# Cross-attention on one Trainium2 core: seven block products in place of eight, values made directly, fixed buffers and a new order

## The chip, the core and the metric

The kernel runs on one core of one Trainium2 chip. The core has five instruction queues that work side by side: PE (TensorE, the matrix multiplier, with its weight loads listed as PEld), DVE (VectorE), ACT (ScalarE), POOL (GpSimd) and SP (SyncE, here only issuing DMA). Matrix products land in PSUM, eight banks of 128 partitions by 512 fp32 values. PE, DVE and ACT reach PSUM in this kernel; POOL works on SBUF alone. Each engine runs its own instructions strictly in the order in which the program lists them, and waits for the other engines through semaphores.

The metric is the device time of one execution in microseconds (us). Three executions of the kernel before took 1933.29, 1933.73 and 1934.09 us, with a median of 1933.73 us.

## The reference

Cut to what matters, with `B = 32` batches, `C = 256` channels and `N = 1024` positions:

```python
x_q = einsum('oc,bcn->bno', w_qk, y)
x_k = einsum('oc,bcn->bon', w_qk, x)
x_v = einsum('oc,bcn->bon', w_v, x) + b_v[None, :, None]
energy = einsum('bnc,bcm->bnm', x_q, x_k)
attention = softmax(energy, axis=-1)
attention = attention / (1e-07 + attention.sum(axis=1, keepdims=True))
x_r = einsum('bcn,bnm->bcm', x_v, attention)
x_r = relu(einsum('oc,bcn->bon', w_t, x - x_r) + b_t[None, :, None])
return x + x_r
```

## The kernel before, in words

**Weights folded once.** The program computes G = w_qk^T w_qk (negated) at the start, so that the keys of a batch are G x and the energies are y^T (G x); and w_t w_v, so that the output projection is folded into the values. All fp32 operands are split into two fp32r parts, HIGH (the rounded value) and LOW (the rest), and every product is three matmuls: HIGH x HIGH, HIGH x LOW, LOW x HIGH (`ORDER`, line 45). ACT writes the HIGH part as a copy, and DVE (if the source is in PSUM) or POOL (if it is in SBUF) writes the LOW part as a subtraction.

**One batch.** With channels as two blocks of 128 (`KC`), positions as two halves of 512 (`MB`) and eight position tiles of 128 (`NT`), a batch consists of these groups of matmuls, each of 128x128 weights against 128x512 columns unless said otherwise:

- `k`, keys G x: 2 output blocks x 2 halves x 2 input blocks x 3 = 24 (`keys`, `channels`, lines 287 to 301).
- `E`, energies: 8 tiles x 2 halves x 2 blocks x 3 = 96 (`energy`, line 357).
- `A`, attention: 8 tiles x 2 channel blocks x 2 halves x 3 = 96 (`attention`, line 413).
- `X`, w_t x: 24 (`straight`, line 339).
- `W`, the mixing of the attention result with w_t w_v: 24 (`mixed`, line 275). In batches 1 to 30 the attention works on x itself, turned to positions-by-channels through a strided load and a transpose on DVE (`load_positions`, `turned_x`, lines 233 to 262), and `W` follows. The first and the last batch have instead values made ahead, `V` (`values`, line 323): 48 matmuls of 128x256.

**Softmax of one tile** (lines 371 to 411): DVE takes the row minimum of the 128x1024 energies in PSUM (`min`), ACT does the exponential in place with the row sum (`exp`), DVE the reciprocal (`ri`), ACT the HIGH part of each half (`h`), DVE the LOW part (`l`) and the column sums (`sum`). At the batch's end DVE reduces the column sums (`cols`, `inv`, `turn`), scales the result (`div`), POOL adds w_t x (`join`), ACT applies ReLU (`pos`), a POOL DMA adds x from HBM (`add`) and an SP DMA stores (`st`).

**PSUM.** Banks are used as four pairs. Energies of successive tiles alternate between two pairs (`place`, line 354), so the next tile is multiplied while the softmax of this one runs; the other two pairs hold the attention result.

**Order.** Nothing reorders the work: the strings `FIRST`, `STEADY` (run for batches 2 to 30) and `STEPS` (lines 724 to 877) list the operations, one word each, and every engine takes its own words in that order. A `+` puts a word one batch ahead, a `-` one batch back.

Of the kernel before, what the change touches and what calls it, by code (L numbers as in the profile page):

```python
# [17 lines left out]
def kernel(  # L18
# [28 lines left out]
    const = ctx.enter_context(tc.tile_pool(name="const", bufs=1))  # L47
    ps_m = ctx.enter_context(tc.tile_pool(name="ps_m", bufs=1, space=bass.MemoryType.PSUM))
    one = ctx.enter_context(tc.tile_pool(name="one", bufs=1))
    yp = ctx.enter_context(tc.tile_pool(name="yp", bufs=3))  # L50
    ep = ctx.enter_context(tc.tile_pool(name="ep", bufs=3))
    rawp = ctx.enter_context(tc.tile_pool(name="rawp", bufs=4))
    xep = ctx.enter_context(tc.tile_pool(name="xep", bufs=3))
    sp = ctx.enter_context(tc.tile_pool(name="sp", bufs=3))
# [20 lines left out]
    banks = ps_m.tile([P, 8, MB], F32, name="banks")  # L75

    def pair(j):
        return banks[:, 2 * j : 2 * j + 2]

# [6 lines left out]
    def accumulate(into, from_):  # L86
        return pool.dma_start(into, from_, accum_op=ALU.add)

    stage = one.tile([P, KC, N], F32, tag="z", name="stage")

    def two(j):
        return stage.rearrange("p k n -> p (k n)")[:, 2 * j * C : 2 * (j + 1) * C].rearrange(
            "p (k c) -> p k c", k=KC
        )  # L100
# [5 lines left out]
    for k, start in enumerate((load, act.dma_start)):  # L106
        start(wqk[:, k], w_qk[ts(k, P)])

    def raw(name):
        return rawp.tile([P, N], F32, tag="raw", name=name)  # L110

    def raw_x(name, b, k, by=load):
        to = raw(f"{name}_{b}_{k}")
        by(to, x[b, ts(k, P)])
        return to

    def y_half(b, half):
        return y[b].rearrange("(k p) n -> p k n", p=P)[:, :, ts(half, MB)]

    x0 = [raw_x("x", 0, 0)]  # L120
    act.dma_start(wt, w_t.rearrange("(k p) c -> p k c", p=P))
    load(wv, w_v.rearrange("(k p) c -> p k c", p=P))
    x0.append(raw_x("x", 0, 1))

    few = const.tile([P, P], F32, name="few")
    zeros = nc.const_aps.tensor(0.0, [P, P], F32)
    parts = const.tile([P, NB, NG + 1], F32, name="parts")
    dve.memset(parts[:, :, NG], EPS)
    sc = const.tile([P, NB, 1], F32, name="sc")
    ubias = const.tile([P, KC, 1], F32, name="ubias")  # L130
    xbias = const.tile([P, KC, 1], F32, name="xbias")
    for _ in range(5):
        pe.matmul(banks[:, 7, :P], zeros, zeros, start=True, stop=True)
    make_identity(nc, ident)

    def positions(name):
        return xep.tile([P, N], F32, tag="xe", name=name)

    works = [positions(f"work_{j}") for j in range(2)]

    def work(j):
        return works[j // 2][:, ts(j % 2, KC * C)]

    def area(j):
        return work(j).rearrange("p (k c) -> p k c", k=KC)

    class Weights:

        def __init__(self, name, p, by):
            self.forms = const.tile([P, FORMS, KC, C], F32R, name=name)  # L150
            self.p, self.by = p, by
            self.h, self.l = (self.forms[:, j] for j in range(FORMS))

        def high(self, at=slice(0, KC)):
            act.mul(self.h[:, at], self.p[:, at], self.by)

        def low(self):
            dve.scalar_tensor_tensor(self.l, self.p, self.by, value(self.h), ALU.mult, ALU.subtract)

    def matmul(into, lhs, rhs, start, stop):  # L160
        pe.matmul(into, lhs, rhs, start=start, stop=stop, skip_group_check=True)

    def late(b):

        return 0 < b < B - 1

    class Queries:

        def __init__(self, q):
            self.b, self.half = divmod(q, MH)  # L170
            self.from_ = raw(f"y_{self.b}_{self.half}")
            load(self.from_.rearrange("p (k n) -> p k n", k=KC), y_half(self.b, self.half))

        def ordered(self, f):

            if late(self.b):
                return f.rearrange("p t k (g j) -> p (k g) t j", j=G32)
            return f.rearrange("p t k n -> p k t n")

        def loaded(self):  # L180
            if late(self.b):
                return self.from_.rearrange("p (h t j) -> p h t j", t=HT, j=G32)
            return self.from_.rearrange("p (k t n) -> p k t n", k=KC, t=HT)

        def high(self):
            self.f = yp.tile([P, FORMS, HT, KC, P], F32R, tag="yf", name=f"yf_{self.b}_{self.half}")
            act.copy(self.ordered(self.f[:, HIGH]), self.loaded())

        def low(self):
            pool.tensor_tensor(  # L190
                self.ordered(self.f[:, LOW]),
                self.loaded(),
                self.ordered(value(self.f[:, HIGH])),
                ALU.subtract,
            )
# [12 lines left out]

    class Batch:

        def __init__(self, b):
            self.b = b
            self.at = b % 2
            self.late = late(b)
            self.row, self.ef, self.uf, self.zf, self.xe = {}, {}, [], [], {}
            self.key_bank, self.x_from, self.xr, self.xp = {}, {}, {}, {}

        def load_x(self, k):
            self.xr[k] = raw_x("x", self.b, k)

        def x_high(self, k):
            if k == 0:
                self.xf = one.tile([P, FORMS, KC, N], F32R, tag="xf", name=f"xf_{self.b}")
            act.copy(self.xf[:, HIGH, k], self.xr[k])

        def x_low(self, k):
            pool.tensor_tensor(
                self.xf[:, LOW, k], self.xr[k], value(self.xf[:, HIGH, k]), ALU.subtract
            )

        def load_positions(self, q):
            self.xp[q] = raw(f"xp_{self.b}_{q}")
            to = self.xp[q].rearrange("p (c n) -> p c n", n=P)
            from_ = x[self.b].rearrange("(c r) n -> r c n", r=G32)
            for g in range(NG):
                load(to[ts(g, G32)], from_[:, :, q * MB + g * P : q * MB + (g + 1) * P])

        def turned_x(self, q):  # L240

            blocks = self.xp[q].rearrange("p (j r) -> p j r", r=G32)
            dve.transpose(blocks, blocks)

        def turned(self, q):
            return self.xp[q].rearrange("p (c t r) -> p t c r", t=HT, r=G32)

        def turned_form(self, q, j):
            return self.uf[q][:, j].rearrange("p (t c r) -> p t c r", t=HT, r=G32)

        def turned_high(self, q):
            u = one.tile([P, FORMS, HT * C], F32R, tag=f"uf{q}", name=f"uf_{self.b}_{q}")
            self.uf.append(u)
            act.copy(self.turned_form(q, HIGH), self.turned(q))

        def turned_low(self, q):
            pool.tensor_tensor(
                self.turned_form(q, LOW),
                self.turned(q),
                value(self.turned_form(q, HIGH)),  # L260
                ALU.subtract,
            )

        def mixed_high(self, k):
            f = ep.tile([P, FORMS, N], F32R, tag="ef", name=f"zf_{self.b}_{k}")
            self.zf.append(f)
            act.copy(f[:, HIGH], flat(pair(2 + k)))

        def mixed_low(self, k):
            f = self.zf[k]
            dve.tensor_tensor(f[:, LOW], flat(pair(2 + k)), value(f[:, HIGH]), ALU.subtract)

        def mixed(self, c, halves=range(MH)):
            for h in halves:
                for j, m in ORDER:
                    for k in range(KC):
                        matmul(
                            pair(3 - c)[:, h],  # L280
                            vw.forms[:, j, k, ts(c, P)],
                            self.zf[k][:, m, ts(h, MB)],
                            (j, m) == ORDER[0] and k == 0,
                            (j, m) == ORDER[-1] and k == KC - 1,
                        )

# [627 lines left out]
```

## Time and profile before

The profiled execution took 1933.57 us; its span, from first to last instruction, is 1931.4 us.

| engine | busy us | share of the span | instructions |
|---|---|---|---|
| PE | 1923.8 | 100% | 8553 |
| PEld | 1595.9 | 83% | 8553 |
| DVE | 1473.3 | 76% | 2083 |
| ACT | 1068.2 | 55% | 1485 |
| POOL | 665.8 | 34% | 331 |

Busy time is the union of an engine's instructions. A line of a group of instructions reads: program line, engine, operation, output<-input, shape, count, then the total busy time, the mean time of one instruction in ns, and the idle time of the engine just before them with what ended it. Matmuls are pipelined, so the mean time of one (389 ns for 512 columns) is longer than the distance between two. All calls go through one helper, so every row has line L67, and the names of the tiles tell the groups apart.

### The profile page before, as it was taken

The page shows a single profiled execution, that of the slowest core. Times are in us where ns is not written, and L with a number is a line of the kernel's source. Part 1 is how long each engine was busy: PE and PEld are TensorE (multiplying, and loading weights), DVE is VectorE, ACT ScalarE, POOL GpSimd, SP SyncE. Part 2 cuts the span into 40 slices and gives each one's busy share as a digit, 9 for nine tenths or more (in the row PEclk, how much of TensorE's full clock was granted, in tenths as well). Part 3 has the DMA queues.
Part 4 walks back from the last instruction along what each step waited for, and adds up shares of the span by engine and source line. Part 5 has one row for each costly group of instructions (what it writes and reads, how often), then busy time and mean ns, then how long its engine had stood idle before and what let it go on. Part 6 is the DMA issues. An engine that isn't in the chain of part 4 may idle for free.

```text
span 1931.4 us, 22944 instructions
## 1 busy us (share of the span) xinstructions
PE 1923.8 (100%) x8553; PEld 1595.9 (83%) x8553; DVE 1473.3 (76%) x2083; ACT 1068.2 (55%) x1485; POOL 665.8 (34%) x331
## 2 busy tenths in 40 slices
PE   9999999999999999999999999999999999999998
PEld 8888888888888888888888888888888888888887
DVE  6877877778777787777877778877778777787776
ACT  6555555555555555555555555555555555555544
POOL 3333234232343333333333333334233342323413
PEclk9999999999999999999999999999999999999999
DMA  4133234332243322434224333233332343322321
GB/s 139 57 97 88 66 88 109 87 98 67 77 109 88 102 66 73 109 88 109 71 63 107 99 98 86 58 97 101 96 88 64 90 109 88 91 63 87 109 55 44
DMA packets 112126, 168.08 MB, mean 87 GB/s; under 512 B 8336, under 2 KB 70928, under 8 KB 112016
## 3 DMA queue, kind: packets, MB, share of 16 engines
q1 hardware_dynamic: 102960, 134.77, 22.8%
q0 software_dynamic: 8640, 31.46, 9.4%
q8 instruction: 67, 1.10, 0.2%
q14 instruction: 43, 0.35, 0.1%
q10 hardware_dynamic: 416, 0.39, 0.1%
HBM read 133.04 MB, written 33.55 MB: 86 GB/s over the span
## 4 chain that ended last, share of the span: by engine, by line
PE 99%; DMA 0%; DVE 0%; issue 0%; ACT 0%
PE banks L67 99%; DMA stage<-in_L_xattn_w_qk_dram 0%; DVE banks L67 0%; DVE z L67 0%; ACT work L67 0%
## 5 line engine op out<-in xcount | busy, mean ns | idle before, releaser
L67 PE MATMUL banks<-ef,uf 128*128 128x512 f32 x3051 | 731.0, 388 | 0.0
L67 PE MATMUL banks<-gf,yf 128*128 128x512 f32 x3072 | 728.6, 389 | 0.0
L67 PEld LDWEIGHTS banks<-gf,yf 128*128 128x128 f32 x3072 | 576.4, 188 | 119.5
L67 PEld LDWEIGHTS banks<-ef,uf 128*128 128x128 f32 x3051 | 571.4, 188 | 118.1
L67 ACT ACTIVATE banks<-banks,nm 128x1024 f32<-128x1024 f32 x256 | 278.7, 1089 | 399.3 <-DVE nm L67 398.8
L67 DVE TENSOR_REDUCE nm<-banks 128x1 f32<-128x1024 f32 x256 | 313.6, 1225 | 209.4 <-PE banks L67 205.9
L67 ACT ACTIVATE ef<-banks,ri 128x512 fp32r<-128x512 f32 x506 | 323.9, 686 | 184.9 <-DVE ri L67 108.8
L67 DVE SCALAR_TENSOR_TENSOR ef<-banks,ri,ef 128x512 fp32r<-128x512 f32 x506 | 370.4, 743 | 13.2 <-ACT ef L67 12.0
L67 POOL TENSOR_TENSOR uf<-xp,uf 128x1024 fp32r<-128x1024 f32 x60 | 144.5, 2409 | 603.9 <-ACT uf L67 597.5
L67 DVE SCALAR_TENSOR_TENSOR acc<-banks,ri,acc 128x512 f32<-128x512 f32 x448 | 327.9, 744 | 5.0 <-ACT ef L67 0.2
L67 POOL TENSOR_TENSOR z<-z,xe 128x1024 f32<-128x1024 f32 (+1 forms) x63 | 150.8, 2394 | 205.0 <-DVE z L67 187.3
L67 POOL TENSOR_TENSOR xf<-x,xf 128x1024 fp32r<-128x1024 f32 x62 | 149.2, 2407 | 168.8 <-ACT xf L67 168.8
L67 PE MATMUL banks<-xf,gw 128*128 128x512 f32 x768 | 189.3, 389 | 0.0
L67 PE MATMUL banks<-xf,tw 128*128 128x512 f32 x768 | 184.3, 389 | 0.0
L67 POOL TENSOR_TENSOR yf<-y,yf 128x1024 fp32r<-128x1024 f32 x64 | 163.7, 2559 | 17.1 <-ACT yf L67 17.1
L67 PEld LDWEIGHTS banks<-xf,tw 128*128 128x128 f32 x768 | 144.1, 188 | 29.9
L67 PEld LDWEIGHTS banks<-xf,gw 128*128 128x128 f32 x768 | 144.1, 188 | 29.8
L67 PE MATMUL banks<-zf,vw 128*128 128x512 f32 x720 | 168.2, 389 | 0.0
L67 PEld LDWEIGHTS banks<-zf,vw 128*128 128x128 f32 x720 | 135.1, 188 | 28.1
L67 DVE TENSOR_TENSOR zf<-banks,zf 128x1024 fp32r<-128x1024 f32 x60 | 73.4, 1225 | 104.9 <-ACT zf L67 104.9
L67 POOL DMA_DIRECT2D z<-in_x_dram x60 | 52.6, 876 | 240.5 <-ACT z L67 240.5
L67 ACT CAST gf<-banks 128x1024 fp32r<-128x1024 f32 x64 | 64.9, 1016 | 100.0 <-PE banks L67 100.0
(76 smaller groups left out, 1001.6 us busy)
## 6 DMA issues: line engine op xcount, KB each, us to landing
x<-in_x_dram SPq DMA_DIRECT2D x64, 512.0 KB, 4.1
y<-in_ctx_dram SPq DMA_DIRECT2D x64, 512.0 KB, 3.9
out_dram<-z SPq DMA_DIRECT2D x62, 512.0 KB, 2.7
xp<-in_x_dram SPq DMA_DIRECT2D x240, 128.0 KB, 3.0
z<-in_x_dram POOLq DMA_DIRECT2D x60, 512.0 KB, 6.6
xo<-in_x_dram SPq DMA_DIRECT2D x4, 512.0 KB, 3.4
out_dram<-z SPq DMA_DIRECT2D x3, 256.0 KB, 2.0
stage<-in_L_xattn_w_t_dram ACTq DMA_DIRECT2D x1, 256.0 KB, 4.8
```

The costliest lines, as they stand in the source:

```text
L67: self.last = getattr(self.engine, name)(*args, **kwargs)
```

## The change

Nearly the whole program is rewritten. What is computed stays the same; these are the parts.

**Seven block products.** Keys, w_t x and energies become chains of seven products of blocks (Strassen's scheme in Winograd's form) in place of eight, each product again three matmuls. For the energies a pair of position tiles p (tiles 2p and 2p+1) is one chain: 2 tiles x 2 channel blocks on the left, 2 channel blocks x 2 halves on the right. The products accumulate in three PSUM banks: bank a takes P1, P6, P7, P4 in turn, bank b P2, bank c P5 and P3. Between them the partial sums of bank a are read out by ACT (`r1` after P1, `r2` after P6, `r3` after P7) and added by DVE into the other banks:

```python
def product(into, left, right, first):
    for i, (j, m) in enumerate(ORDER):
        matmul(into, left(j), right(m), first and i == 0, i == len(ORDER) - 1)
...
def chain(name, bank, left, right):
    where = {1: "a", 2: "b", 5: "c", 6: "a", 7: "a", 4: "a", 3: "c"}
    for i, w in where.items():
        words[f"{name}P{i}"] = lambda b, i=i, w=w: product(
            banks[:, bank[w]], left(i), right(i), i in (1, 2, 5)
        )
...
KB = dict(a=2, b=0, c=1)
...
XB = dict(a=6, b=4, c=5)
...
EB = dict(a=2, b=0, c=1, d=3)
...
def energy_read(b, p, j):
    act.copy(rs["e", b, p, j], eb["a"])

def energy_block(b, p, j, w, to, least, first):
    dve.tensor_tensor_reduce(
        out=eb[to], in0=eb[w], in1=rs["e", b, p, j], scale=1.0,
        scalar=LARGE if first is None else small[first, b, p],
        op0=ALU.add, op1=ALU.min, accum_out=small[least, b, p],
    )

def energy_least(b, p):
    dve.tensor_reduce(small["mD", b, p], eb["a"], AX.X, ALU.min)
    dve.tensor_tensor(small["m1", b, p], small["mD", b, p], small["mB", b, p], ALU.min)

def tile_banks(n):
    return banks[:, EB["a"] : EB["a"] + 2] if n % 2 else banks[:, EB["b"] : EB["b"] + 2]
...
word(f"E{p}c11", energy_block, p, 1, "b", "b", "mA", None)
word(f"E{p}c22", energy_block, p, 3, "c", "d", "mB", None)
word(f"E{p}c12", energy_block, p, 2, "c", "c", "m0", "mA")
word(f"E{p}m21", energy_least, p)
```

So `c11` is bank b plus r1, `c22` is bank c plus r3 written to bank d, `c12` is bank c (after P3) plus r2; the row minimum comes out of the same instructions and of `m21`, which reduces bank a and combines two columns of one value per row (`m1`). Tile 2p lies in banks 0 and 1, tile 2p+1 in banks 2 and 3, and every pair of every batch, and the keys (`KB`), use these same banks. Attention, values and w_t x use banks 4 to 7.

**Operands.** Left and right operands of the seven products are four blocks as they are and sums of blocks. The sums are made before the split: on POOL for x (`xT1` to `xT4`) and y (`ys1` to `ys4` of each half), on DVE and POOL for the keys (`kT1`, `kT3`, `kT4` and `kT2`). Their HIGH parts are further ACT copies (`xTh`, `ysh`, `kTh`) and their LOW parts further POOL subtractions (`xTl`, `ysl`, `kTl`); the key blocks' own HIGH and LOW (`khD`, `klD`) are an ACT copy and a POOL subtraction, since `kc11` and `kc22` put them in SBUF. For the weights this is done once (`left_blocks`), for G on DVE, for w_t on POOL.

**Values.** Every batch makes `V` (48 matmuls of 128x256), split by `vh` on ACT and `vl` on DVE. The turned load, its transpose and `W` are gone.

**Buffers.** Pools that rotate are replaced by one tile per buffer: one set of x, y, key and value operands, one z and one xe (w_t x), two raw input tiles, four attention tiles (`efs`), four tiles of sums and four of reads (`rs`).

**Order.** New strings. The steady one, for batch b, begins and goes on:

```
+xTl1 +yl01 +ys13 sum61 A400 A511 +kr1 h61 +kP6 +ysl0 +ys12 sum60 l60 +kr2 +kP2
l61 +kP7 +kP5 A700 -add0 +yl00 +ys14 h71 +kr3 +kP4 cols +kc11 +kc22 +kP3 l71 A600
+kc12 +khD +kT1 +kT3 A410 A501 A411 A710 A401 +kTh0 +kh21 +ysh1 +klD +kT2 +kTl0
inv +kT4 +kl21 turn A711 A610 +kTh1 A611 A701 +E0P1 +E0P2 +E0r1 +kTl1 +yl11 +E0P6
A601 +E0r2 +E0P7 -st0 +E0P5 div1 +E0c11 div0 +E0r3 +yh10 +E0c22 +E0P4 +E0P3 +E0m21
+V10 +yl10 +V11 +E0c12 join1 +exp1 +ri1 +exp0 +V00 +h10 +sum10 +sum11 +ri0 +l10
+h00 +E1P1 +l00 +vh1 ++ldx0 +sum01 +h11 +ysl1 +E1r1 +V01 +h01 +vl1 +vh0 +sum00
+E1P6 +xP1 +E1r2 ++ldx1 +E1P2 join0 ++xT3 +l11 +E1P7 +l01 +E1P5 +xr1 ++xh0 +E1r3
+vl0 +xP6 pos1 +E1c11 +E1P4 +E1c22 +xr2 +xP2 +E1m21 +exp3 +xc11 +E1P3 +E1c12 +ri3
+xP5 +A100 +h30 ++xl0 add1 ++xT1 +sum30 +exp2 +l30 +xP7 +A111 +sum31 +E2P1 +A011
...
+E2c22 +E2m21 +E2c11 +exp5 +ri5 +A101 +A311 +E2P3 +A000 +h50 +sum50 +l50 +E3P1
++xTh0 +A001 +E2c12 +h51 +E3r1 +exp4 ++ys01 ++xT2 ++ys03 +sum51 ++xT4 +A310 +E3P6
+ri4 +h41 +sum41 ++xl1 +A210 +A300 +E3r2 +E3P7 ++xTl0 ++ys02 ++ys04 ++xTh1 +h40
+A211 +l41 +sum40 +l51 +l40 +E3P5 +E3r3 +E3P4 +E3P2 +E3c22 ++ldy1 +E3P3 +A510
+E3m21 pos0 +E3c11 ++yh00 ++ysh0 +E3c12 +A301 +exp7 +ri7 +A200 +h70 +A201 ++ys11
+sum70 +l70 +exp6 ++yh11 +sum71 +A500 ++kP1 +ri6 st1 +h60
```

The start and the end are new too. The keys of the first batch, which ran as soon as G was there (`first_keys`), now come after the blocks of both weights, the bias product and the sums of x:

```
ldx0 ldx1 xT1 xh0 xl0 xT2 xh1 xl1 xT4 xTh1 xT3 xTl1 xTh0 xTl0 V00 V11 kP1 ldy0 kr1
kP6 V10 kP5 ldy1 yh11 kr2 yh01 ys01 kP2 kP7 kr3 ys03 yh00 kc22 kc11 V01 kP3 kP4
yl01 ys02 khD yl00 kc12 kT1 ys04 klD kh21 vh1 vh0 ysh0 kT3 vl1 kT2 kT4 kTh0 kl21
kTh1 vl0 E0P2 +ldx0 ysl0 kTl1 xP1 E0P1 xP2 xP5 E0r1 yh10 xr1 E0P6 xP6 kTl0 E0r2
...
```

The special last batch (`STEPS` with its `end_` functions, which split the last piece, kept x in SBUF and stored in pieces of 192 to 512 columns) is replaced by the steady operations in a short string:

```
A511 A501 A410 A411 A400 h71 A710 -add0 h61 sum60 sum61 l71 cols l60 inv l61 -st0
A711 A401 A700 A610 A611 A701 A601 turn A600 div1 div0 join1 join0 pos1 add1 pos0
st1 add0 st0
```

More of the change, by code (lines that the diff above doesn't have):

```diff
@@ new lines, with matmul @@
+    raws = Ring("raws", 2, [N])
+    sums = Ring("sums", 4, [2, MB])
+    efs = Ring("efs", 4, [FORMS, MH, MB], F32R)
+    rs = Ring("rs", 4, [MB])
+    small = Ring("small", 60, [1])
+    parts = mem.tile([P, NB, NG + 1], F32, name="parts")
+    sc = mem.tile([P, NB, 1], F32, name="sc")
+    ubias = mem.tile([P, KC, 1], F32, name="ubias")
+    xbias = mem.tile([P, KC, 1], F32, name="xbias")
+    wtb = mem.tile([P, KC], F32, name="wtb")
+    def matmul(into, lhs, rhs, start, stop):
+        pe.matmul(into, lhs, rhs, start=start, stop=stop, skip_group_check=True)
@@ L122 @@
[L122 to L133, printed above, removed]
@@ L160, in matmul @@
[L160 to L195, printed above, removed]
@@ L609 @@
[L609 to L621 removed]
+    zeros = nc.const_aps.tensor(0.0, [P, P], F32)
+    dve.memset(parts[:, :, NG], EPS)
@@ L622 @@
+    for _ in range(5):
+        pe.matmul(banks[:, 7, :P], zeros, zeros, start=True, stop=True)
+    make_identity(nc, ident)
+    gram(pair(2), wqk)
+    act.mul(graw[:, 0], pair(2)[:, 0, :C], -1.0)
+    act.mul(graw[:, 1, P:], pair(2)[:, 1, P:C], -1.0)
+    pe.transpose(pair(2)[:, 1, :P], graw[:, 0, P:], ident)
+    act.copy(graw[:, 1, :P], pair(2)[:, 1, :P])
+    left_blocks("g", gws, graw, dve)
     for i in range(KC):
@@ new lines @@
+    word("kc22", key_block, 3, "c", 1)
+    word("kc12", key_block, 2, "c", None)
+    word("kh21", lambda b: act.copy(g(HIGH, K21), kb["a"]))
+    word(
+        "kl21",
+        lambda b: dve.tensor_tensor(g(LOW, K21), kb["a"], value(g(HIGH, K21)), ALU.subtract),
+    )
+    word("kT1", key_sum, ("k13", 0), "c", ("k", 0))
+    word("kT3", key_sum, ("k13", 1), "c", ("k", 1))
+    word(
+        "kT2",
+        lambda b: pool.tensor_tensor(
+            sums["k24", b][:, 0], sums["k", b][:, 1], sums["k13", b][:, 0], ALU.subtract
+        ),
+    )
@@ new lines, with columns @@
+    for n in range(NT):
+        word(f"exp{n}", exp, n)
+        word(f"ri{n}", recip, n)
+        for h in range(MH):
+            word(f"h{n}{h}", high, n, h)
+            word(f"l{n}{h}", low, n, h)
+            word(f"sum{n}{h}", share, n, h)
+            for c in range(KC):
+                word(f"A{n}{c}{h}", attention, n, c, h)
+    def columns(b):
+        dve.tensor_reduce(
+            parts[:, :, 0],
+            acc.rearrange("p (j r) -> p j r", r=G32),
+            AX.X,
+            ALU.add,
+            apply_transpose=True,
+        )
@@ new lines, in divided, with joined, relu, added @@
+    def divided(b, c):
+        dve.scalar_tensor_tensor(z[:, c], flat(pair(2 + c)), ubias[:, c], rc, ALU.add, ALU.mult)
+    def joined(b, c):
+        pool.tensor_tensor(z[:, c], z[:, c], xe[:, c], ALU.add)
+    def relu(b, c):
+        act.activation(z[:, c], z[:, c], AF.Relu)
+    def added(b, c):
+        pool.dma_start(z[:, c], x[b, ts(c, P)], accum_op=ALU.add)
+    def stored(b, c):
+        load(out[b, ts(c, P)], z[:, c])
+    word("cols", columns)
+    word("inv", inverse)
+    word("turn", inverse_turned)
@@ new lines @@
+    """
+    STEADY = """
+        +xTl1 +yl01 +ys13 sum61 A400 A511 +kr1 h61 +kP6 +ysl0 +ys12 sum60 l60 +kr2 +kP2
+        l61 +kP7 +kP5 A700 -add0 +yl00 +ys14 h71 +kr3 +kP4 cols +kc11 +kc22 +kP3 l71 A600
+        +kc12 +khD +kT1 +kT3 A410 A501 A411 A710 A401 +kTh0 +kh21 +ysh1 +klD +kT2 +kTl0
+        inv +kT4 +kl21 turn A711 A610 +kTh1 A611 A701 +E0P1 +E0P2 +E0r1 +kTl1 +yl11 +E0P6
+        A601 +E0r2 +E0P7 -st0 +E0P5 div1 +E0c11 div0 +E0r3 +yh10 +E0c22 +E0P4 +E0P3 +E0m21
+        +V10 +yl10 +V11 +E0c12 join1 +exp1 +ri1 +exp0 +V00 +h10 +sum10 +sum11 +ri0 +l10
+        +h00 +E1P1 +l00 +vh1 ++ldx0 +sum01 +h11 +ysl1 +E1r1 +V01 +h01 +vl1 +vh0 +sum00
+        +E1P6 +xP1 +E1r2 ++ldx1 +E1P2 join0 ++xT3 +l11 +E1P7 +l01 +E1P5 +xr1 ++xh0 +E1r3
+        +vl0 +xP6 pos1 +E1c11 +E1P4 +E1c22 +xr2 +xP2 +E1m21 +exp3 +xc11 +E1P3 +E1c12 +ri3
+        +xP5 +A100 +h30 ++xl0 add1 ++xT1 +sum30 +exp2 +l30 +xP7 +A111 +sum31 +E2P1 +A011
+        +ri2 +xr3 +sum21 +xP4 +xc22 ++ldy0 +E2r1 +E2P6 +h21 +h20 +l21 +sum20 +xP3 +E2r2
+        +h31 +E2P7 +xw21 +E2P5 +xc12 +E2r3 +A110 ++yh01 ++xh1 +l31 +l20 +E2P4 +E2P2 +A010
+        +E2c22 +E2m21 +E2c11 +exp5 +ri5 +A101 +A311 +E2P3 +A000 +h50 +sum50 +l50 +E3P1
+        ++xTh0 +A001 +E2c12 +h51 +E3r1 +exp4 ++ys01 ++xT2 ++ys03 +sum51 ++xT4 +A310 +E3P6
+        +ri4 +h41 +sum41 ++xl1 +A210 +A300 +E3r2 +E3P7 ++xTl0 ++ys02 ++ys04 ++xTh1 +h40
+        +A211 +l41 +sum40 +l51 +l40 +E3P5 +E3r3 +E3P4 +E3P2 +E3c22 ++ldy1 +E3P3 +A510
+        +E3m21 pos0 +E3c11 ++yh00 ++ysh0 +E3c12 +A301 +exp7 +ri7 +A200 +h70 +A201 ++ys11
+        +sum70 +l70 +exp6 ++yh11 +sum71 +A500 ++kP1 +ri6 st1 +h60
```

920 lines of the change are left out of this document (321 added, 599 removed).

## The prediction

> **What bounds the kernel now.** I read the page's head first, then the chain that ended last, the waits of PE, and the windows.
>
> ```profile
> span 1931.4 us, 22944 instructions
> PE 1923.8 (100%) x8553; PEld 1595.9 (83%) x8553; DVE 1473.3 (76%) x2083; ACT 1068.2 (55%) x1485; POOL 665.8 (34%) x331
> 5.86 1919.26 PE banks L67 x8535
> PE banks L67 <- DMA stage<-in_L_xattn_w_qk_dram: 0.3, 1, 0.3
> 19.50:1911.00 1891.50, 1891.50 (x8371) 1567.22 (x8370) 1453.99 (x2058) 1052.85 (x1464) 652.95 (x316) 1.00 0.32 86
> ```
>
> The chain that ended last is one run of matmuls from 5.86 us to the end, and after the start no engine makes PE wait. So fewer matmuls are worth their full time, as long as the other engines keep up. A matmul's price is read from distances, not from its mean of 389 ns:
>
> ```profile
> 13.75 5.92 PE L67 MATMUL banks<-vw,xf 128*128 128x256 f32 x48
> 19.50 5.63 PE L67 MATMUL banks<-gf,yf 128*128 128x512 f32 x24
> L67 PE MATMUL banks<-gf,yf 128*128 128x512 f32 x3072 | 728.6, 389 | 0.0
> ```
>
> The 48 matmuls of 256 columns fill 13.75 to 19.50: 5.75 us. The window 19.50:1911.00 holds 8371 records, 48 of them the last batch's V: (1891.50 - 5.75) / 8323 = 0.2266 us for 512 columns, so 0.68 us for a product of three. Check: 30 batches x 264 x 0.2266 + 2 x (240 x 0.2266 + 5.75) = 1915 us; the remaining 16 us of the span are the start and the end.
>
> **PE after the change.** The seven-product chains take E from 96 to 84, k and X from 24 to 21 each; W's 24 (5.44 us) become V's 5.75. A batch is (84 + 96 + 21 + 21) x 0.2266 + 5.75 = 56.06 us against 59.83: 32 batches are 1794 us, 121 less. That is all the change can win; the rest of this part is what it gives back.
>
> **The other engines.**
>
> ```profile
> L67 DVE SCALAR_TENSOR_TENSOR acc<-banks,ri,acc 128x512 f32<-128x512 f32 x448 | 327.9, 744 | 5.0 <-ACT ef L67 0.2
> L67 DVE TENSOR_TENSOR z<-banks,xe 128x512 f32<-128x512 f32 x2 | 1.4, 692 | 0.1
> L67 DVE TENSOR_REDUCE nm<-banks 128x1 f32<-128x1024 f32 x256 | 313.6, 1225 | 209.4 <-PE banks L67 205.9
> L67 DVE TENSOR_TENSOR gf<-banks,gf 128x1024 fp32r<-128x1024 f32 x64 | 78.2, 1224 | 41.5 <-ACT gf L67 41.4
> L67 DVE TRANSPOSE_TENSOR_REDUCE parts<-acc 128x32 f32<-128x1024 f32 x32 | 39.9, 1247 | 1.0
> L67 DVE STREAM_TRANSPOSE rc<-sc 128x1024 f32<-128x1024 f32 x32 | 39.5, 1235 | 0.0
> L67 DVE TENSOR_REDUCE parts<-parts 32x32 f32<-32x32 f32 x93 | 19.7, 212 | 1.8
> L67 DVE RECIPROCAL sc<-sc 32x32 f32<-32x32 f32 x31 | 10.6, 341 | 1.1
> L67 DVE SCALAR_TENSOR_TENSOR z<-banks,ubias,rc 128x1024 f32<-128x1024 f32 x62 | 79.2, 1279 | 39.7 <-PE banks L67 39.4 <-issue 0.2
> L67 DVE RECIPROCAL ri<-rs 128x1 f32<-128x1 f32 x256 | 40.7, 159 | 18.0 <-ACT banks L67 8.4
> 29.71 1.40 DVE L67 SCALAR_TENSOR_TENSOR ef<-banks,ri,ef 128x512 fp32r<-128x512 f32 x2
> L67 ACT CAST gf<-banks 128x1024 fp32r<-128x1024 f32 x64 | 64.9, 1016 | 100.0 <-PE banks L67 100.0
> L67 ACT COPY wtT<-banks 128x512 f32<-128x512 f32 x1 | 0.6, 588 | 0.1
> L67 ACT ACTIVATE ef<-banks,ri 128x512 fp32r<-128x512 f32 x506 | 323.9, 686 | 184.9 <-DVE ri L67 108.8 <-DVE acc L67 42.2 <-PE banks L67 33.6
> L67 ACT ACTIVATE banks<-banks,nm 128x1024 f32<-128x1024 f32 x256 | 278.7, 1089 | 399.3 <-DVE nm L67 398.8
> L67 ACT ACTIVATION_READ_ACCUMULATOR banks<-banks,nm 128x1 f32 x256 | 49.9, 195 | 0.0
> L67 POOL TENSOR_TENSOR xf<-x,xf 128x1024 fp32r<-128x1024 f32 x62 | 149.2, 2407 | 168.8 <-ACT xf L67 168.8
> L67 POOL TENSOR_TENSOR tw<-wtT,tw 128x512 fp32r<-128x512 f32 x1 | 1.3, 1301 | 1.8 <-ACT tw L67 1.8
> ```
>
> The add that also takes a minimum (`c11`, `c22`, `c12`) is not in this trace. Below, it costs the plain add, 0.69; above, an add and a half reduction one after the other, 0.69 + 0.61 = 1.30. I take 0.74, the row of the two-operand DVE operation with a per-row scalar, which it resembles most. DVE per batch, from rows of lone instructions: 12 x 0.74 for the energies, 4 x (0.69 + 0.16) for `m21`, 10 x 0.69 for keys and w_t x, 32 x 0.744 for `l` and `sum`, and 10.4 for two vl of 1.22, two div of 1.28, cols 1.25, turn 1.24, eight ri of 0.16 and some 1.6 for the small ones of inv: 53.4 us. Two in a row take 1.40 and not 1.49, so back to back it is nearer to 47.5. The same count gives ACT 49 (12 reads of 0.59 for the energies alone, thirteen 1024-wide copies near 1.03) and POOL 44 (eleven 1024-wide operations of 2.4, seven 512-wide of 1.3, ten of 256 columns at some 0.7, two DMA issues). PE stays the longest at 56, but the margin of DVE falls from 14 us a batch to 3 to 9.
>
> **Reads that PE must wait for.** P6 overwrites what r1 reads, so P1, r1, P6, r2, P7, r3, P4 are a chain. One link costs PE's tail 0.389 - 0.227 = 0.16, 0.03 to start, 0.59 of copy, and 0.14 until PE runs again:
>
> ```profile
> 5.73 0.14 issue
> ```
>
> In all, 0.92 us. Where two or more products stand between in the PE order, 1.36 us cover it, and what follows is on time. Five links have only one, 0.68 us: P1-P6, P6-P7 and P7-P4 of E0, P6-P7 of E2, P6-P7 of the keys. 5 x 0.24 = 1.2 us a batch.
>
> **Banks that are not doubled.** Every pair of tiles uses banks 0 to 3, so E1P1 waits until h, l and sum of tile 1 are done. From the end of E0P4: tail 0.19, m21 0.69 + 0.16, exp 1.28, the second exp 1.28, h 0.69, l 0.74, restart 0.14 = 5.2 us; PE has P3 and three parts of V in the meantime, 0.68 + 4.31 = 5.0 us. The same walk over the four queues in the steady order gives E2P1 0.2 us late and E3P1 0.1 us late, and kP1 on time. So these stages are balanced to some tenths; I book 0.6 us. The key chain runs through POOL: from the end of kP7 r3 0.8, kc22 0.7, khD 1.0, klD 2.4, kT2 1.3, kTl0 2.4 and kTl1 2.4 follow each other, 11 us with the gaps, until the second matmul of E0P6; PE has 16 products before it, 10.9 us, and what E0's link adds. On time by a hair, nothing booked; if it is late, by 1 us or less.
>
> Together 1.8 us a batch: a period of 57.9, 54 us over 30 batches. Walked with lone durations (no overlap between two instructions) the stalls are 3.5 us; with everything covered but E0's links, 0.7.
>
> **Start and end.**
>
> ```profile
> x<-in_x_dram SPq DMA_DIRECT2D x64, 512.0 KB, 4.1
> z<-in_x_dram POOLq DMA_DIRECT2D x60, 512.0 KB, 6.6
> out_dram<-z SPq DMA_DIRECT2D x62, 512.0 KB, 2.7
> L67 POOL DMA_DIRECT2D z<-in_x_dram x60 | 52.6, 876 | 240.5 <-ACT z L67 240.5
> L67 ACT ACTIVATE z<-z 128x1024 f32<-128x1024 f32 x62 | 65.9, 1065 | 0.0
> 1924.61 0.50 PE L67 MATMUL banks<-ef_last,uf 128*128 128x192 f32 x3
> 1926.39 0.33 SPq L486 DMA_DIRECT2D out_dram<-z  x1
> ```
>
> Before, keys and V (24 x 0.2266 + 5.75 = 11.2 us) are done at 19.50: 8.3 us lost. After, POOL is a queue: w_t's blocks and the bias product until about 15 (ACT's xh0 stands behind that bias), then xT1, xl0 to 20.5, xT2, xl1 to 24, where the first V matmul that needs it can go, xT4, xT3, xTl1 to 29, xTl0 to 31.5; the keys end near 36. y's sums, klD, kT2, ysl0, kTl1 and kTl0 on POOL hold E0P7 to about 48, E0 ends at 50 with 18 us of PE work done: 32 lost, and the first softmaxes, with little beside them, cost some 5 more. I take 37 (25 if half of the POOL queue hides, 45 if it does not at all). The end: after A600, div0 1.3, join0 2.4, pos0 1.1, the adding DMA 0.9 + 6.6 and the store: 12 us until its issue, plus 5 as now (1926.4 to 1931.4): 17 against 6.3 after the last matmul.
>
> **Sum:** 1794 + 54 + 37 + 17 = 1902 us of span. The profiled execution took 1933.57 with a span of 1931.4; with the same 2.2 outside it, 1904 us (that execution lies 0.2 from the median of 1933.73). Stalls of 0.7 to 3.5 us (21 to 105 us) and the start's bounds make 1868 to 1945 for this case.
>
> **Rival 1, slower: m1 stands behind POOL.** `m1`, the small `tensor_tensor` of `m21`, is the only DVE operation of the steady loop with two tensor inputs in SBUF; all others have one in PSUM. Should it have to wait for a running POOL instruction, exp and all of the bank chain above move with it, and that chain has no slack. By the walk, POOL is then in ysl1, xl1 and yl01 in three of the four pairs: 2.0, 1.9 and about 0.6 us, 4.5 us a batch: 1904 + 30 x 4.5 = 2040; if the phases fall at random (79% busy, 1 us left on average, four times), 3 us, 1990. From 1 us a batch on (30 us) it turns the gain into a loss. Against it: no row here shows such a wait. For it: nothing in this trace excludes it, since DVE's only operations with two SBUF inputs run at the start with POOL idle:
>
> ```profile
> 6.28 1.22 DVE L67 TENSOR_TENSOR xf<-x,xf 128x1024 fp32r<-128x1024 f32 x1
> 9.14 1.23 DVE L67 TENSOR_TENSOR xf<-x,xf 128x1024 fp32r<-128x1024 f32 x1 [1.03 <-ACT xf L67]
> 11.02 2.39 POOL L67 TENSOR_TENSOR yf<-y,yf 128x1024 fp32r<-128x1024 f32 x1 [9.70 <-ACT yf L67]
> ```
>
> The Trainium skill, "SBUF — State Buffer", section "Who interferes with whom", states just this: a DVE instruction with two SBUF inputs contends with a GpSimd instruction that reads SBUF, and the second to issue blocks until the first has finished; by that rule the time would be the 1990 to 2040 of this rival and not 1904. No run here shows it for an operand of one value per row.
>
> **Rival 2: DVE becomes the bound.** If the add with minimum costs 1.0 rather than 0.74, DVE's 47.5 to 53.4 become 51 to 57 and c22 and c12, both in the bank chain, put 0.5 on each pair: 2 us a batch, 1904 + 60 = 1965; at 1.30 it is 2040. At 0.85 it is 0.9 a batch, 1930: no change. For it: between E1P1 and E2P1 the order lists 11.0 us of PE work and 12.3 of DVE by lone rows.
>
> **How the numbers follow.** Forecast 0.58, rival 1 0.27, rival 2 0.15. The 1868 to 1945 of the forecast hold nearly all of its 0.58; reaching to 2005 adds most of rival 2 and half of rival 1, so some 0.16 is left out. What can be told from no change is 0.2%, 4 us: faster takes 0.52 of the forecast's 0.58, a third of rival 2 and little of rival 1, 0.58; the same 0.05; slower 0.37.
>
> **What would show it.** Right: a period of 57 to 59 us between two E0P1, PE waits on ACT reads of 0.2 to 0.3 us at the five named links, the first E0 done near 50 us, A600 some 17 us before the end, DVE busy near 85%. Rival 1 shows as an `m1` of 0.5 to 2.4 us in place of 0.16 and PE waits on l or sum at E1P1 and E3P1. Rival 2 shows in the mean of the add with minimum. The forecast is wrong if PE waits for POOL's kTl0, kTl1 or klD in every batch, or if the period passes 59.8.

## The result and the profile after

The changed kernel takes 2215.31 us (median of 4 executions, 2212.97 to 2221.73) against 1933.81 before: 1.146 times as long, 95% interval 1.144 to 1.149. It is slower by 281 us, where 1904 was forecast. The head of its page:

```profile
span 2219.9 us, 25140 instructions
PE 1978.3 (89%) x8671; PEld 1552.5 (70%) x8671; DVE 1718.9 (77%) x3049; ACT 1431.0 (64%) x2227; POOL 1401.6 (63%) x974
PEclk8999999999999999999999999999999999999998
```

PE is no longer busy all the time, and no other engine has taken its place: DVE is at 77%. A kernel with four engines at 63 to 89% is bound by waits between them, so the waits are the next view (who waited for what, total us, times, longest):

```profile
ACT banks L62 <- DVE small L62: 246.8, 127, 3.6
DVE acc L62 <- ACT efs L62: 184.7, 189, 1.7
PE banks L62 <- ACT efs L62: 144.7, 59, 2.9
PEld banks L62 <- ACT rs L62: 73.1, 171, 1.9
```

`small` is the minimum before exp, `efs` written by ACT is h and by DVE l, `acc` the column sums, `rs` the reads r1 to r3. So PE waits most at the hand-over of a bank pair to the next products. The row puts this wait down to h, the last event before the restart; but the h that ended last reads another bank (h00 before E1P1, h51 before E3P1), and E1P1, E2P1, E3P1 and kP1 start 0.15 us after the end of l10, l30, l50 and l70, in every steady batch. l comes late because h and the sums before it came late, these because exp came late, and exp waits for `small`. The groups of DVE that touch `small` and the new add with minimum, each in its own form:

```profile
L62 DVE TENSOR_TENSOR small<-small 128x1 f32<-128x1 f32 x128 | 138.7, 1083 | 4.4
L62 DVE CUSTOM_DVE_ANT_0 banks<-banks,rs 128x512 f32<-128x512 f32 x256 | 176.5, 694 | 48.5 <-PE banks L62 35.5
L62 DVE CUSTOM_DVE_ANT_0 banks<-banks,rs,small 128x512 f32<-128x512 f32 x128 | 96.2, 751 | 5.1
L62 DVE DVE_READ_ACCUMULATOR2_ANT small<- 128x1 f32 x384 | 53.7, 140 | 0.0
```

The first row is `m1`: one value per row, 1083 ns on average. Now one hand-over in order of time, E0 of batch 15 to E1P1 (start, duration, engine; idle time in brackets):

```profile
1071.09 0.69 DVE L62 TENSOR_REDUCE small<-banks 128x1 f32<-128x512 f32 x1
1071.12 2.40 POOL L62 TENSOR_TENSOR z<-z,xe 128x1024 f32<-128x1024 f32 x1
1071.82 1.71 DVE L62 TENSOR_TENSOR small<-small 128x1 f32<-128x1 f32 x1
1073.47 2.40 POOL L62 TENSOR_TENSOR ysum<-sums,ysum 128x1024 fp32r<-128x1024 f32 x1
1073.57 1.09 ACT L62 ACTIVATE banks<-banks,small 128x1024 f32<-128x1024 f32 x1 [3.22 <-DVE small L62]
...
1075.76 0.68 ACT L62 ACTIVATE efs<-banks,small 128x512 fp32r<-128x512 f32 x1
...
1076.48 1.41 DVE L62 TENSOR_SCALAR acc<-banks,small 128x512 f32<-128x512 f32 x2 [1.51 <-ACT efs L62]
...
1077.87 0.73 DVE L62 SCALAR_TENSOR_TENSOR efs<-banks,small,efs 128x512 fp32r<-128x512 f32 x1
...
1078.75 0.92 PE L62 MATMUL banks<-gf,yd 128*128 128x512 f32 x3 [2.46 <-ACT efs L62]
```

Two things are to be seen. `m1` starts beside a POOL instruction (1071.12 to 1073.52) and ends at 1073.53, with it. And the sums (acc) stand idle for 1.51 us until ACT's h of the same bank is done, though they need nothing that h makes; l follows the sums and E1P1 follows l. E1P1 runs 2.46 us late. The next pair but one shows what long waits cost besides:

```profile
1104.17 1.01 PE L62 MATMUL banks<-gf,yd 128*128 128x512 f32 x3 [2.81 <-ACT efs L62]
1104.98 2.76 PE L62 MATMUL banks<-efs,uf 128*128 128x512 f32 x6
1107.54 1.22 PE L62 MATMUL banks<-gf,ysum 128*128 128x512 f32 x3
```

After the wait of 2.81 us before E3P1, the six matmuls after it take 2.76 us in place of 1.52, 427 ns from one to the next: half speed. A wait of nearly this length does not always do so. E1P1 waits as long in two other batches, and the twelve matmuls of V01 after it run at half speed in the first and at full speed in the second:

```profile
804.32 1.44 PE L62 MATMUL banks<-gf,yd 128*128 128x512 f32 x3 [2.47 <-ACT efs L62]
805.56 2.65 PE L62 MATMUL banks<-vws,xf 128*128 128x256 f32 x12
873.53 0.94 PE L62 MATMUL banks<-gf,yd 128*128 128x512 f32 x3 [2.48 <-ACT efs L62]
874.30 1.58 PE L62 MATMUL banks<-vws,xf 128*128 128x256 f32 x12
```

The period, from one E0P1 to the next, is 67.6 us here (1065.18 to 1132.75), against 57.9 forecast and 59.8 in the kernel before.

### The profile page after: what moved, and what is told of

It reads as the page before. It is cut to its first block, busy times and chain, and to the rows that moved or that the text cites. A ratio compares the mean times of both kernels' runs of the same rounds, so it can differ in the third digit from the quotient of the medians.

```text
span 2219.9 us, 25140 instructions
## 1 busy us (share of the span) xinstructions
PE 1978.3 (89%) x8671; PEld 1552.5 (70%) x8671; DVE 1718.9 (77%) x3049; ACT 1431.0 (64%) x2227; POOL 1401.6 (63%) x974
## 5 line engine op out<-in xcount | busy, mean ns | idle before, releaser
L62 PE MATMUL banks<-efs,uf 128*128 128x512 f32 x3072 | 801.6, 401 | 1.3 <-DVE efs L62 1.3
L62 PEld LDWEIGHTS banks<-efs,uf 128*128 128x128 f32 x3072 | 597.4, 195 | 134.1 <-DVE efs L62 2.2
L62 PE MATMUL banks<-gf,yd 128*128 128x512 f32 x1152 | 347.5, 421 | 184.3 <-ACT efs L62 144.7
L62 ACT COPY rs<-banks 128x512 f32<-128x512 f32 x480 | 283.0, 590 | 265.4 <-PE banks L62 264.9
L62 DVE SCALAR_TENSOR_TENSOR acc<-banks,small,acc 128x512 f32<-128x512 f32 x448 | 334.8, 747 | 142.7 <-ACT efs L62 139.3
L62 PE MATMUL banks<-gf,ysum 128*128 128x512 f32 x1536 | 442.6, 407 | 1.5 <-DVE acc L62 0.3
L62 ACT ACTIVATE banks<-banks,small 128x1024 f32<-128x1024 f32 x256 | 278.0, 1086 | 246.9 <-DVE small L62 246.8
L62 ACT ACTIVATE efs<-banks,small 128x512 fp32r<-128x512 f32 x512 | 350.0, 692 | 114.0 <-DVE small L62 108.0
L62 DVE SCALAR_TENSOR_TENSOR efs<-banks,small,efs 128x512 fp32r<-128x512 f32 x512 | 369.7, 743 | 17.3 <-ACT efs L62 17.2
L62 PEld LDWEIGHTS banks<-gf,ysum 128*128 128x128 f32 x1536 | 283.9, 193 | 110.3 <-ACT rs L62 42.5
```

The costliest lines, as they stand in the source:

```text
L62: self.last = getattr(self.engine, name)(*args, **kwargs)
```

## The experiments

The table has, for the steady batches, how much later than at full rate a product came (us, mean of the batches), then the median period and the time:

| kernel | E0's links and E0P3 | E1P1 | E2P1 | E3P1 | E3P2 | kP1 | E2P7, kP7 | period | time |
|---|---|---|---|---|---|---|---|---|---|
| forecast | 0.7 | 0.2 | 0.2 | 0.1 | 0 | 0 | 0.5 | 57.9 | 1904 |
| changed kernel | 1.16 | 2.95 | 0.84 | 2.77 | 0.49 | 0.85 | 0.40 | 67.6 | 2215 |
| e1_one_input | 1.16 | 1.16 | 0.83 | 0.89 | 0.88 | 0.48 | 0.40 | 62.4 | 2051 |
| e3_sums_first | 1.16 | 0.02 | 0.83 | 0.89 | 0.89 | 0.48 | 0.55 | 61.3 | 2018 |
| e6_sums_elsewhere | 1.15 | 0.02 | 0.11 | 0.17 | 0 | 0 | 0.54 | 58.4 | 1928 |

### m1 with one input, and the sums first

The first edit puts the two minima into neighbouring columns and reduces them:

```diff
+    mins = Ring("mins", 8, [2])
...
-            accum_out=small[least, b, p],
+            accum_out=mins[b, p][:, 0:1] if least == "mB" else small[least, b, p],
...
-        dve.tensor_reduce(small["mD", b, p], eb["a"], AX.X, ALU.min)
-        dve.tensor_tensor(small["m1", b, p], small["mD", b, p], small["mB", b, p], ALU.min)
+        dve.tensor_reduce(mins[b, p][:, 1:2], eb["a"], AX.X, ALU.min)
+        dve.tensor_reduce(small["m1", b, p], mins[b, p], AX.X, ALU.min)
```

> m1 is made by a reduction over two neighbouring columns, one input in SBUF, in place of the two-input tensor_tensor; all else is the changed kernel. Theory LOCK (m1 waits for the POOL instruction that is running, and this is the miss): m1's 1.08 us mean falls to about 0.2, the waits of PE before E1P1 and E3P1 of 2.7 and 3.0 us fall below 1 us, the half-speed matmuls behind the longest wait go, period from 67.5 to about 60, time about 1970 to 2000. Theory TURNS (DVE and ACT reads of one PSUM bank run one after the other in program order, so sum waits for h: 185 us of DVE idle time in the changed kernel's waits; the m1 wait only fills time that DVE would wait anyway): m1 falls too, but the time falls by less than 60 us, to 2155 or more.

Measured: 2051.41 us (1.061 of the kernel before, 1.059 to 1.062), 164 us less than the changed kernel. The group of m1 in e1_one_input (its busy time, and the mean ns of one):

```profile
L62 DVE TENSOR_REDUCE small<-mins 128x1 f32<-128x2 f32 x128 | 19.9, 155 | 4.4
```

A window of about two batches of e1_one_input, 1000 to 1140 us, with busy time and count of PE, PEld, DVE, ACT and POOL, then the mean granted clock, the DMA share and GB/s:

```profile
1000.00:1140.00 140.00, 133.19 (x602) 104.48 (x603) 110.54 (x213) 99.99 (x158) 98.11 (x69) 1.00 0.25 73
```

and the same window of the changed kernel:

```profile
1000.00:1140.00 140.00, 126.39 (x558) 99.08 (x557) 110.82 (x195) 89.86 (x140) 89.29 (x62) 0.96 0.22 61
```

m1 falls from 1083 to 155 ns, the granted clock returns from 0.96 to 1.00, and no half-speed matmuls are left in the steady batches. The time lies between the two forecasts, 1970 to 2000 and 2155 or more: LOCK is right that m1 cost most of the miss, and wrong that it was the whole: 62.4 us a batch, not 60.

The second edit, on top of the first, is in the order alone:

```diff
-+h10 +sum10 +sum11 +ri0
+ +sum10 +sum11 +h10 +ri0
-+h30 ++xl0 add1 ++xT1 +sum30 +exp2 +l30 +xP7 +A111 +sum31 +E2P1
+ +h30 ++xl0 add1 ++xT1 +sum31 +exp2 +l30 +xP7 +A111 +sum30 +E2P1
-+h50 +sum50 +l50 +E3P1 ... +sum51
+ +h50 +sum51 +l50 +sum50 +E3P1 ...
-+h70 +A201 ++ys11 +sum70 +l70 +exp6 ++yh11 +sum71
+ +h70 +A201 ++ys11 +sum71 +l70 +exp6 ++yh11 +sum70
```

> As e1_one_input, and sum10 and sum11 stand before h10 in the order, and in the pairs of tiles 3, 5 and 7 the column sum of the other half (sum31, sum51, sum71) comes first, while ACT's h works on this half's bank. LOCK: nothing is left to gain here, within 20 us of e1_one_input. TURNS: about 1.4 us in the first pair and 0.3 to 0.7 in each of the others, 45 to 100 us less than e1_one_input, and DVE's wait for h falls from 185 us to below 100.

Measured: 2018.23 us, 33 us less than e1_one_input, between the 20 of LOCK and the 45 of TURNS. The wait of the sums for h falls from

```profile
DVE acc L62 <- ACT efs L62: 164.5, 189, 1.6
```

in e1_one_input to

```profile
DVE acc L62 <- ACT efs L62: 49.3, 70, 1.6
```

in e3_sums_first. E1P1's loss is gone, as TURNS has it (1.16 to 0.02); the other three pairs gained nothing. There the sums were no longer late, but h, sum and l of one half still follow each other, in whatever order, before the bank is free: E2P1, E3P1 and kP1 now start 0.15 us after the sum of that half, which has come to stand behind l.

### The wait of a two-input operation by itself

The kernel before got one operation more per tile, on the way from the minimum to exp, once with two inputs in SBUF, once with one:

```diff
             dve.tensor_reduce(low, flat(self.place(n)), AX.X, ALU.min)
-            self.row[n] = low
+            again = sp.tile([P, 1], F32, tag="ag", name=f"ag_{self.b}_{n}")
+            dve.tensor_tensor(again, low, low, ALU.min)        # b_two_inputs
+            dve.tensor_reduce(again, low, AX.X, ALU.min)       # b_one_input
+            self.row[n] = again
```

> The kernel before with one operation more per tile: the row minimum combined with itself by a two-input tensor_tensor of one column, on the way to exp. LOCK: POOL is busy 34% of the span with instructions of 2.4 us, so some third of the 256 last up to 2.4 us, each ending within 0.05 us of the POOL instruction's end, and the others 0.16; mean about 0.5. The time changes by less than 0.5% since the energies are double there. TURNS or a plain cost of small operations: all near 0.16 whatever POOL does.

> The control: the same column through a reduction with one input. LOCK: all near 0.16 to 0.2, also beside POOL. If a small operation of any kind waits behind POOL, these are as long as those of b_two_inputs.

The group in b_two_inputs:

```profile
L67 DVE TENSOR_TENSOR ag<-nm 128x1 f32<-128x1 f32 x256 | 140.4, 548 | 8.8
```

and in b_one_input:

```profile
L67 DVE TENSOR_REDUCE ag<-nm 128x1 f32<-128x1 f32 x256 | 39.3, 154 | 8.8
```

Of the 256 with two inputs, the 161 that start while POOL is idle last 159 to 164 ns; the 95 that start beside a POOL instruction that reads SBUF end, in the median, 15 ns after it ends, the longest after 2161 ns. With one input all last 153 to 156 ns. The forecast of a mean of 0.5 holds. That the time would not change does not: b_two_inputs takes 1971.87 us, 1.019 of the kernel before (1.017 to 1.021), and b_one_input 1934.05, 1.000 (0.999 to 1.001). Even with energies that are double in PSUM, 0.39 us more per tile on this path costs 38 us.

### What is left: DVE's load, or the turns of the banks

e5_no_sums leaves out the column sums of all tiles but tile 1, and with them the second normalisation in effect. e6_sums_elsewhere leaves them out too, but puts a reduction over SBUF in the place of each, so that DVE has the same to do in the same order:

```diff
         p, a = tile_banks(n)[:, h], acc[:, ts(h, MB)]
+        if n != 1:
+            dve.tensor_reduce(small["x", b, n, h], a, AX.X, ALU.add)   # e6 alone
+            return
         if n == 1:
```

> e3_sums_first without the column sums of all tiles but tile 1 (so the second normalisation is left out in effect): 14 DVE operations of 0.74 us fewer per batch. Theory TURNS (what is left is that h on ACT, sum and l on DVE read one bank in turn, so each hand-over of banks to PE is one sum later than booked): the waits of PE before E2P1, E3P1, E3P2 and kP1, 3.0 us a batch together, shrink to below 1, period 61.3 to about 58.5 to 59.3, time 1930 to 1955. Theory LOAD (DVE has too much to do): the same fall, since its load goes too; the next run tells the two apart. Theory LINKS (reads r1 to r3 with one product of cover are the rest): less than 20 us.

> e3_sums_first with each of these 14 sums replaced by a reduction of 512 SBUF values in the same place of DVE's order: the load of DVE stays nearly (0.6 to 0.69 for 0.74), but the operation reads no PSUM bank; the column sums are left out again. TURNS: most of the fall of e5_no_sums stays, 1940 to 1975. LOAD: within 20 us of e3_sums_first, 2000 to 2020.

Measured: 1927.96 and 1927.89 us, 0.997 of the kernel before (0.996 to 0.998 both), 2 and 12 us below the ranges that TURNS gave. DVE's groups and PE's waits of e6_sums_elsewhere:

```profile
L62 DVE TENSOR_REDUCE small<-acc 128x1 f32<-128x512 f32 x448 | 297.7, 673 | 0.0
```

```profile
PEld banks L62 <- ACT rs L62: 80.4, 196, 1.1
PEld banks L62 <- DVE efs L62: 22.5, 63, 4.3
```

DVE does 448 operations of 673 ns in place of 448 of 747, and the time is that of the kernel without them. So LOAD is out: it is not the work of the sums but their reading of the PSUM bank, in turn with h and l, that cost 90 us of e3_sums_first. What remains on PE is what the forecast had booked, the reads (rs) and little else: a period of 58.4.

### One effect beside the other

e10_sums_m1_two is the changed kernel with the second edit alone; e11_elsewhere_m1_two is e6_sums_elsewhere with m1 as in the changed kernel (column sums left out again).

> The changed kernel with the sums' order of e3_sums_first alone, m1 still a two-input operation. If the two effects add, 33 us less than the changed kernel, about 2183. If m1's wait stands in the same place as the sums' waits, less than 10 or more than 60.

> e10 with the sums of all tiles but tile 1 replaced by reductions of SBUF values, as in e6_sums_elsewhere (column sums left out): the changed kernel with the bank turns of the sums gone and the wait of m1 left. If the wait of m1 has its price by itself, the 3.0 to 4.5 us a batch that were worked out for it, 2020 to 2075; if it costs only where the sums have used up all slack, below 1970; if it costs more than its own length in any case, above 2090.

Measured: 2133.62 and 2007.18 us. The wait of m1 is then worth 2215 - 2051 = 164 us in the order of the change, 2134 - 2018 = 115 with the sums first, and 2007 - 1928 = 79 with the sums off the banks: 5.1, 3.6 and 2.5 us a batch. So the two effects do not add: e10 would then be at 2182 and e11 at 1928 + 164 = 2092. The 2007 of e11 lies outside all three ranges that were given for it.

Two things account for it. First, m1 does not wait equally long, since POOL's instructions stand differently beside it. The group of m1 in e10 and in e11 (1083 ns in the changed kernel):

```profile
L62 DVE TENSOR_TENSOR small<-small 128x1 f32<-128x1 f32 x128 | 132.7, 1036 | 4.4
L62 DVE TENSOR_TENSOR small<-small 128x1 f32<-128x1 f32 x128 | 112.9, 882 | 4.4
```

Beyond 155 ns, 128 of them wait 119, 113 and 93 us. Second, the half rate: summed over the matmuls that started in a stretch of half granted clock, the distances beyond full rate come to 62 us in the changed kernel, 9 in e10, 2 in e11 and none in e1, e3 and e6 (steady batches). Without these, the three prices are 102, 106 and 77 us, 83 to 94% of m1's wait. This is an estimate from the traces, since PE might have waited for part of the lost time anyway. By it, nearly all of m1's wait falls on the time in each of the three kernels, and what makes it dearest in the changed one is the half rate.

### Order, key chain, start

e7_order, from e3_sums_first:

```diff
-+sum30 +E2P1 +A011
+ +sum30 +A011 +E2P1
-+sum50 +E3P1 ++xTh0 +A001 +E2c12
+ +sum50 +A001 +E3P1 ++xTh0 +E2c12
-+h41 +sum41 ... ++xTh1 +h40 +A211 +l41 +sum40 +l51 +l40
+ +h41 +sum40 +sum41 ... +h40 ++xTh1 +A211 +l41 +l51 +l40
-+E3P3 +A510 ... +E3c12 +A301
+ +E3P3 +A301 ... +E3c12 +A510
```

> e3_sums_first in another order: A011 before E2P1 and A001 before E3P1 (a product in the place of the wait), sum40 before h40, h40 before xTh1, l40 without sum40 ahead of it, A301 before A510. If the period is the chain of bank hand-overs plus PE work that stands at the wrong place, E2P1 and E3P1 give 0.4 each, E3P2 0.9: 1.5 to 2 us a batch, 45 to 60 us, time 1958 to 1975. If another engine's load bounds it, less than 20 us.

Measured: 1974.31 us (1.021, 1.019 to 1.023), 44 us less than e3_sums_first, at the lower edge of what was expected. E3P2's 0.89 went; at E2P1 and E3P1 the moved product fills the wait, but it had been the second cover of a read, so that E2P6 and E3P6 now come 0.27 us late, behind r1, and E3P7 loses 0.44 in place of 0.11.

e9_cover_e0, from e7_order:

```diff
-A711 A610 +kTh1 A611 A701 +E0P1 +E0P2 +E0r1 +kTl1 +yl11 +E0P6 A601 +E0r2
+A711 A610 +kTh1 +E0P1 +E0P2 A611 +E0r1 +kTl1 +yl11 +E0P6 A601 A701 +E0r2
```

> e7_order with two attention products moved into E0: A611 between E0P2 and E0P6, A701 between A601 and E0P7, so that the reads r1 and r2 of E0 have two products of cover. Theory LINKS (a read with one product of cover costs 0.27 us, and nothing else holds E0): both waits go, 0.54 us a batch, 17 us less than e7_order, about 1957. Theory KEYS (the key chain through POOL ends within 0.2 us of the moment at which E0P6 needs kTl1, so what is taken from in front of it comes back as a wait for POOL): E0P6 waits some 0.8 us for kTl1 instead of r1, only r2's 0.27 is won, 5 to 9 us, about 1967.

Measured: 1984.21 us, 10 us more than e7_order. The waits of PE and of its weight loads in e9_cover_e0:

```profile
PE banks L62 <- POOL gf L62: 11.8, 30, 0.4
```

```profile
PEld banks L62 <- POOL gf L62: 24.5, 30, 0.8
```

E0P6 now waits for kTl1 from POOL in each of 30 batches (0.67 us where r1 had cost 0.28); E0P7's link of 0.32 is won. KEYS was right about the place. Both theories missed the sign, because E0P1 is late as well: it now comes earlier in PE's order and starts 0.15 us after the end of kl21 in every batch, the last read of the bank that it overwrites, 0.22 us late. So 0.28 and 0.32 were given for 0.67 and 0.22, some 0.3 us a batch or 9 of the 10 us.

e8_head_on_dve, from e7_order: the first batch's x sums and LOW parts, and w_t's blocks, on DVE in place of POOL.

```diff
-    left_blocks("t", tws, wtT, pool)
+    left_blocks("t", tws, wtT, dve)
...
-        pool.tensor_tensor(into, left, right, ALU.subtract)
+        (pool if b else dve).tensor_tensor(into, left, right, ALU.subtract)
```

> e7_order with the sums and LOW parts of x of the first batch and the blocks of w_t made on DVE in place of POOL (1.22 against 2.4 us for 1024 columns, 0.69 against 1.3 for 512). If the start is POOL's queue as predicted, V00 ends some 7 us and the first E0P1 some 10 us earlier, time 8 to 14 us less than e7_order; if the later POOL work (klD, kTl) holds the first E0 alone, less than 4.

Measured: 1969.92 us (1.018, 1.017 to 1.020), 4.4 us less than e7_order. V00 ends at 23.5 in place of 25.2 and E0P3 at 49.8 in place of 52.0: 2 us, not 10 (kernels with the same start as e7 differ by as much: V00 ends at 27.3 in e6). The gain in time lies between the two forecasts, 8 to 14 and less than 4. So x's operands were only a small part of the start's loss, and most of it stays unexplained in detail. Of the variants of the change that leave nothing out this is the fastest, and it does not reach the kernel before.

## Why the prediction was wrong

**PE work: right.** Products stand at 0.68 us from one to the next and a part of V at 1.44, in every variant wherever nothing waits. The 121 us are really saved.

**Two terms of the sum failed.** `m1` stood in it at 0.16 us, with no wait for POOL; it lasts 1.08 on average, and that is 164 us, half-rate matmuls included (Rival 1 below). The other term is the hand-over of banks, 123 us.

**The hand-over of banks.** I booked 0.6 us a batch for banks that are not doubled, "E2P1 0.2 us late and E3P1 0.1 us late, and kP1 on time". The chain of that walk has exp, h and l but no sum, as if DVE could sum beside ACT's exp and h. The program lets the two engines read one bank only in turn. In the changed kernel none of the 512 sums overlaps the h of its own half, while 96 overlap the h of the tile's other half, in the next bank. So it was in the kernel before as well, and a row that I had quoted says so, h's own, with 42.2 us of idle time ended by `DVE acc`. There it was idle time off the path. Here each pair's bank waits for h, sum and l one after the other. From the forecast's period of 57.9 to e1's 62.4 it is 4.5 us, of which e6 takes back 4.0, or 123 us. The Trainium skill, "PSUM — Partial Sum Buffer", section "PSUM bank collisions raise a hardware error", gives the reason why such turns are needed, since two engines that access one bank at a time collide; no run here lets them overlap.

**Rival 1: right, with a chance of 0.27 that was too small.** m1 waits for POOL's running instruction: it lasts 1.68, 0.29, 1.81 and 0.56 us on average in pairs 0 to 3, so 3.7 us a batch beyond its own 0.16, where 4.5 were worked out for three of the pairs. Only xl1 was the instruction that the walk had placed there (24 of 32 in pair 2); in pair 0 it was join1, not ysl1 (30 of 32), and in pair 3 ys13, not yl01 (29 of 32). That the lengths come near is in part luck. This rival gave 1990 to 2040, 86 to 136 us on top of the forecast. The nearest thing that was run, e11, takes 2007, but only 79 more than e6, as m1 waits 2.9 us a batch there. In the changed kernel it waits 3.7, and costs 164 us with the half-rate matmuls behind it, which this rival did not have. The rule of the Trainium skill that stood beside it ("SBUF — State Buffer", section "Who interferes with whom") is shown by b_two_inputs and b_one_input, for one value per row too. I gave it little weight because no row of the trace showed it; but no row could have, and a stated rule that the trace cannot contradict deserved at least even odds.

**Rival 2: wrong.** The add with minimum costs 0.69 (0.75 for c12) and another 0.14 for the read of its accumulator, 0.83 to 0.89 where 0.74 was taken. Yet DVE's load decides nothing: e6 with it and e5 without it take the same time.

**Links: right.** The five links were booked at 0.24 each; those of E0 measure 0.28 to 0.32 and E2P7 0.27; kP7 has 0.13 in the changed kernel and 0.27 from e3 on. What was not booked is 0.24 at E0P3, which waits for c22 and its accumulator read.

**Key chain: right.** "On time by a hair": E0P6 finds kTl1 ready in the changed order, and e9, which takes 1.36 us from in front of it, makes it wait.

**Start: too low. End: right.** E0P3 ends at 53.6 us, not 50, and E1P1 follows at 59.1, in the changed kernel's timeline:

```profile
52.64 0.96 PE L62 MATMUL banks<-gf,ysum 128*128 128x512 f32 x3
59.08 1.65 PE L62 MATMUL banks<-gf,yd 128*128 128x512 f32 x3 [5.48 <-DVE efs L62]
```

E0P1 of the next batch starts at 112.7 with 58 us of PE work before it: 55 us lost, where 37 were taken and 45 was the bound. Up to the end of E0 it is 36, with 32 forecast; the other 19, with 5 forecast, fall on the rest of the first batch, where m1 and the banks have their price too: in e6 they are 8, and the whole start 44. The cause was placed too early in POOL's queue of x, as e8 shows; what else the start loses stays open. The last matmul ends 16.0 us before the end of the span, 17 forecast.

Together: with one input for m1 and the sums off the banks, e6 takes 1928 where 1904 was forecast. Of the 24 us, 15 are 0.5 us a batch (E0P3 and the dearer links), and the rest lies mostly in the start (44 for 37).

## What to carry to other kernels

When work that was double-buffered is made to share one set of buffers, write the chain from the last producer to the next overwrite as a list and add every reader of that buffer in turn: readers on different engines that seem independent may be ordered among themselves, and the trace shows it as idle time before one of them even where it costs nothing yet. A small operation is not cheap by its size: on DVE, with two SBUF operands, it inherits the rest of the SBUF-reading instruction that POOL is running, so combine small values with one operand in SBUF. Waits on one chain do not simply add: taking one away moves what the other waits for, and long waits of PE can bring half-rate matmuls. So price the second one with the first one in place.

## What the runs showed of the hardware

- A DVE `tensor_tensor` of one value per row with both inputs in SBUF lasted 159 to 164 ns with POOL idle and up to 2.4 us beside POOL, ending 15 to 17 ns after POOL's instruction (medians of b_two_inputs and the changed kernel); a one-input reduction stayed at 153 to 158. Beside POOL's issue of a DMA the two-input operation waited for nothing either: 30 of `m1` in the changed kernel, 158 to 163 ns.
- After a wait of PE of 2.81 us, matmuls of 512 columns came 427 ns apart in place of 227, eight of them. The granted clock of the changed kernel is 0.5 in stretches of 3.4 us: 41 of PE's 56 waits of 2.25 to 2.93 us before E1P1 and E3P1 were followed by one, 15 were not, and of the 30 before E1P1, all 2.46 to 2.48 us, 16 were. In e10 it was 5 of 24 such waits (2.2 to 2.9 us), and after the waits of 1.1 us before E1P1 in e10 and e11 none of 60. So in this range the length of the wait alone does not decide. The Trainium skill, "TensorE: Matmul & The Clock Gate", Part 1, states half rate after an idle window of about 3.4 us; the rate agrees, and here shorter waits were at times enough.
- A product that restarts after a wait loses twice: E0P6's first matmul came 158 ns late and its second another 114.
- The add with minimum (694 ns) is followed by a separate read of its accumulator of 140 ns, in DVE's queue and ahead of the consumer.
